# A transformer block with a dynamic convolution on one core: a second norm's squares on another engine, and two taps behind a variance

## The chip, the cores and the metric

The kernel runs on one core of one Trainium2 chip. The metric is the device time of one execution in microseconds. The time before is 3081.14 us, the median of three runs (3079.3 to 3084.65). The core's engines appear in profiles as PE (TensorE, matrix products; PEld are its weight loads), DVE (VectorE), ACT (ScalarE), POOL (GpSimd) and SP (SyncE, which issues the transfers here).

## The reference

The input is 16 images of 192 channels and 56 x 56 points, float32. Two layers follow each other. The first is a shifted-window transformer block, the second a depthwise convolution whose weights depend on the image:

```python
# layer 0, per point over the 192 channels
h = _ln(x, norm1_g, norm1_b)                 # first norm
h = attention in shifted 7 x 7 windows       # qkv, scores + bias + mask, softmax, values, projection
x1 = shortcut + h
y = _ln(x1, norm2_g, norm2_b)                # second norm: mean and variance over the channels
y = gelu(y @ fc1_w + fc1_b) @ fc2_w + fc2_b
x = x1 + y
# layer 1, per image
wt = (relu(bn(mean(x) @ w1.T)) @ w2.T + b2) * MASK      # four taps are left of the 3 x 3
out = depthwise_conv(x, wt) + bias
```

A norm needs, for each point, the sum over the channels and the sum of their squares.

## The kernel before

An image is worked off in four row groups of 2 x 7 rows, called steps, and the loop is pipelined: in loop step `i` the attention of step `i`, the MLP of step `i - 2`, the first norm's sums of step `i + 3` and the convolution of an older image run side by side. 128 channels lie on the partitions of one tile, the other 64 in a second tile (both row halves, one on each half of the partitions).

The sums over channels are matmuls with a selecting matrix (`st`). So that one matmul for each statistic is enough, the three pieces of the data are folded into one before: `own` is what already lies on the right partitions, the rest is copied over by two transfers into `xs[:, 1]`. The same for the squares, `s1` (the 64 channels), `s0[p, 0]` (own) and `s0[:, 1]` (copied):

```python
    def norm_folded(key, i, side):
        v0, v1 = flat_of(i)
        ...
        def copies():
            nc.sync.dma_start(xs[0:64, 1], v0[64:128, 0])
            nc.sync.dma_start(xs[64:128, 1], v0[0:64, 1])

        def sums():
            for p, h in own:
                nc.gpsimd.tensor_tensor(xs[p, 0], v0[p, h], v1[p], ALU.add)              # L274
            nc.gpsimd.tensor_tensor(xs[:, 0], xs[:, 0], xs[:, 1], ALU.add)               # L275

        def squares(engine):
            if engine is nc.gpsimd:
                nc.gpsimd.tensor_tensor(s1, v1, v1, ALU.mult)                            # L279
            else:
                nc.scalar.activation(s1, v1, AF.Square)                                  # L281
            return [
                lambda: [nc.scalar.activation(s0[p, 0], v0[p, h], AF.Square) for p, h in own],  # L283
                lambda: nc.scalar.activation(s0[:, 1], xs[:, 1], AF.Square),             # L284
            ]

        def fold():
            nc.gpsimd.tensor_tensor(s0[:, 0], s0[:, 0], s1, ALU.add)                     # L288
            nc.gpsimd.tensor_tensor(s0[:, 0], s0[:, 0], s0[:, 1], ALU.add)               # L289
```

The variance of both norms, made of the statistics in a PSUM bank pair:

```python
    def norm_vars(keys, st, tag="dev"):
        ...
        nc.scalar.activation(part, st[lo:hi, 0, :T], AF.Square)                          # L323
        nc.vector.tensor_tensor(part, st[64 + lo : 64 + hi, 0, :T], part, ALU.subtract)  # L324
```

The MLP's first layer has six groups of hidden channels on four bank pairs. Groups 0 to 2 take their wide products (128 channels) first and then the narrow ones (64 channels); groups 3 to 5 the other way round. `st` takes the bank pair of group 2, groups 4 and 5 those of 0 and 1, so each waits for the GELU that empties its bank pair:

```python
        for f in range(3):
            take(f); long(dsts[f], wf1, cols(f), y0, True)
        for f in range(3):
            short(dsts[f], wf1, cols(f), y1, False)
            gelu(f)                                                                      # L640
        after()
        for f in range(3, NFC):
            take(f); short(dsts[f], wf1, cols(f), y1, True)
        between()
        for f in range(3, NFC):
            long(dsts[f], wf1, cols(f), y0, False)
            gelu(f)
```

A convolution piece is begun by ScalarE with one tap and finished by VectorE with three (`tap` is L750). An image has six pieces, in four loop steps: one, two, two, one:

```python
    def conv_begin(b, wt, n, y=None):
        ...
        nc.scalar.activation(y, up, AF.Identity, bias=cb[kc], scale=wt[:, kc, 1:2])      # L742

    def conv_rest(b, wt, n, y, part=None):
        ...
        if part != 1:
            tap(0, y[:, :, 1:], up[:, :, : IMG - 1])
        if part == 0:
            return
        tap(2, y[:, :, : IMG - 1], up[:, :, 1:])
        if n in (3, 5):
            nc.vector.tensor_copy(...)                                                   # L762
        tap(3, y[:, :, 1:], cur[:, :, : IMG - 1])
        conv_store(b, n, y)
```

The loop step, cut to what the change touches and what stands around it (`first` is true in the step with an image's first piece, whose weights have only just been made):

```python
    for i in range(2, NS + 2):
        first = bool(convs) and not convs[0]["n"]
        cs = conv_ready(1 if first else 2)
        ys = [] if first else [conv_begin(*c) for c in cs[:1]]
        if has(i + 1):
            norm1_scale(i + 1, dvs.pop(0), nc.vector)        # win <- x, dv: L365, L373

        def after():
            ys.extend(conv_begin(*c) for c in cs[len(ys) :])
            for k, (c, y) in enumerate(zip(cs, ys)):
                conv_rest(*c, y, 0 if k else None)

        def between():
            st = banks(f"st_{i}", C)
            keys.update(stats_of(i, st))
            if keys:
                var.append(norm_vars(keys, st)[0])
            for c, y in zip(cs[1:], ys[1:]):
                conv_rest(*c, y, 1)
        ...
        mlp_first(i - 2, yns.pop(i - 2), hid, (A, B_, C, D, A, B_), after, between)
        ...
        top, share = attention_scores(i, *qs.pop(i), (C, D, A, B_))   # sc, and e <- sc, bias_t: L521
        qs[i + 1], outs = attention_qk(i + 1, C, D, A)                # pq, pe, pk
        ...
        if has(i):
            residual(i, pp, pair1, at)
            copies, sums_, squares, fold = norm_folded(f"2_{i}", i, 1)   # second norm
            copies()
            rest = squares(nc.gpsimd)
            sums_()
        if has(i + 1):
            v_whole()
            attention_v_out(pvs)                             # vbd <- pv on VectorE and ScalarE: L493
        if has(i):
            for f in rest:
                f()
            fold()
```

Of the kernel before, what the change touches and what calls it, by code (L numbers as in the profile page):

```python
# [9 lines left out]
AF = mybir.ActivationFunctionType  # L10
ALU = mybir.AluOpType
# [25 lines left out]
def tile_swin_then_dynamic_conv(  # L37
# [31 lines left out]
    nc = tc.nc  # L69
# [163 lines left out]
    def flat_of(i):  # L233
        v0, v1 = rows_of(i)
        return v0.rearrange("p h r c -> p h (r c)"), v1.rearrange("p r c -> p (r c)")
# [23 lines left out]
    def norm_folded(key, i, side):  # L259


        v0, v1 = flat_of(i)
        xs = one.tile([128, 2, T], F32, tag=("xs", "o")[side], name=f"xs_{key}")
        s0 = one.tile([128, 2, T], F32, tag=f"sq0{side}", name=f"sq0_{key}")
        s1 = one.tile([128, T], F32, tag=f"sq1{side}", name=f"sq1_{key}")
        own = [(slice(h * 64, h * 64 + 64), h) for h in range(2)]
# [8 lines that stand above are left out]
            nc.gpsimd.tensor_tensor(xs[:, 0], xs[:, 0], xs[:, 1], ALU.add)  # L275

        def squares(engine):
            if engine is nc.gpsimd:
                nc.gpsimd.tensor_tensor(s1, v1, v1, ALU.mult)  # L279
            else:  # L280
                nc.scalar.activation(s1, v1, AF.Square)  # L281
            return [
                lambda: [nc.scalar.activation(s0[p, 0], v0[p, h], AF.Square) for p, h in own],  # L283
                lambda: nc.scalar.activation(s0[:, 1], xs[:, 1], AF.Square),  # L284
            ]

        def fold():
            nc.gpsimd.tensor_tensor(s0[:, 0], s0[:, 0], s1, ALU.add)  # L288
            nc.gpsimd.tensor_tensor(s0[:, 0], s0[:, 0], s0[:, 1], ALU.add)  # L289

        xss[key] = xs[:, 0], s0[:, 0]
        return copies, sums, squares, fold
# [438 lines left out]
    def piece_of(b, n):  # L731


        kc, lo = (0, n * PR) if n < 4 else (1, (n - 4) * PR)
        xk = images[b][kc]
        return kc, lo, xk[:, lo : lo + PR], xk[:, lo + 1 : lo + 1 + PR]
# [8 lines left out]
    def conv_rest(b, wt, n, y, part=None):  # L745

        kc, _, up, cur = piece_of(b, n)

        def tap(t, dst, src):
            nc.vector.scalar_tensor_tensor(  # L750
                dst, src, wt[:, kc, t : t + 1], dst, ALU.mult, ALU.add
# [9 lines that stand above are left out]
            p = slice(0, 128) if kc == 0 else slice(64, 128)  # L761
            nc.vector.tensor_copy(  # L762
                y[p, LAST - 3 * PR, :], cb[kc][p].broadcast_to([p.stop - p.start, IMG])
            )
        tap(3, y[:, :, 1:], cur[:, :, : IMG - 1])
        conv_store(b, n, y)
# [37 lines left out]
    def conv_ready(k):  # L804

        ready = []
        while k and convs and "wt" in convs[0]:
            c = convs[0]
            ready.append((c["b"], c["wt"], c["n"]))
            c["n"] += 1  # L810
            k -= 1
            if c["n"] == 6:
                convs.pop(0)
        return ready
# [35 lines left out]
    for h in range(2):  # L850
        p = slice(h * 64, h * 64 + 64)
# [140 lines left out]
    for h in range(2):  # L992
        p = slice(h * 64, h * 64 + 64)
# [77 lines left out]
    v_whole()  # L1071
    copies, sums_, squares, fold = norm_folded("1_4", 4, 0)
    copies()
    for f in squares(nc.scalar):
        f()
    sums_()
    yns[0] = norm2_scale(0, dvs.pop(1), True)
    fold()
# [5 lines left out]
    residual(1, pp, pair1)  # L1084
    copies, sums_, squares, fold = norm_folded("2_1", 1, 1)
    copies()
    for f in squares(nc.gpsimd):
        f()
    sums_()
    fold()  # L1090
    nc.vector.reciprocal(s, s)
    nc.vector.tensor_tensor(s, s, g, ALU.mult)
# [10 lines left out]
    for i in range(2, NS + 2):  # L1103
        A, B_, C, D = pairs
        keys = {}
# [7 lines that stand above are left out]
            norm1_scale(i + 1, dvs.pop(0), nc.vector)  # L1113

        def after():
            ys.extend(conv_begin(*c) for c in cs[len(ys) :])
            for k, (c, y) in enumerate(zip(cs, ys)):
                conv_rest(*c, y, 0 if k else None)

        if (i + 3) % STEPS == 0 and (i + 3) // STEPS < B:  # L1120
            b = (i + 3) // STEPS
            images[b] = load_x(b, nc.sync)

        def between():
            st = banks(f"st_{i}", C)
            keys.update(stats_of(i, st))
            if keys:
                var.append(norm_vars(keys, st)[0])
            for c, y in zip(cs[1:], ys[1:]):
                conv_rest(*c, y, 1)  # L1130

        var = []
        hid = one.tile([128, NFC, 2, T], F32, tag="hid", name=f"hid_{i - 2}")
        mlp_first(i - 2, yns.pop(i - 2), hid, (A, B_, C, D, A, B_), after, between)
        for part in var:
            table(AF.Sqrt)
            norm_root(part)

        if has(i + 3):
            copies, sums_, squares, fold = norm_folded(f"1_{i + 3}", i + 3, 0)  # L1140
            copies()


        outs = [lambda: None] * 4
        if has(i):
            table(AF.Exp)
            top, share = attention_scores(i, *qs.pop(i), (C, D, A, B_))
        if has(i + 1):
            qs[i + 1], outs = attention_qk(i + 1, C, D, A)
        if has(i):  # L1150
            top(0)
        outs[0]()
        if has(i):
            top(1)
            share(0)
        outs[1]()
        if has(i):
            top(2)
            share(1)
        outs[2]()  # L1160
        if has(i):
            top(3)
            share(2)
        outs[3]()
        if has(i):
            share(3)
        for part in var:
            nc.vector.reciprocal(part, part)
            dvs.update(norm_spread(keys, part))

        prts = []

        def turn(f):
            for wp in ((), (), (), (0,), (1,), (2, 3))[f]:
                if has(i):
                    prts.append(attention_turn(i, wp, (C, A)[wp % 2]))

        pf = mlp_wide(i - 2, hid, B_, turn)  # L1180
        mlp_out(i - 2, 0, pf[:, :, :T])
        table(AF.Gelu)
        if has(i + 3):
            sums_()
        if 1 in keys:
            yns[i - 1] = norm2_scale(i - 1, dvs.pop(1), i == NS)
        if has(i):
            o = attention_rows(i, attention_values(i, prts, D, C))
        if has(i + 3):
            for f in squares(nc.scalar):  # L1190
                f()
            fold()
        pf1 = mlp_narrow(i - 2, hid, A)
        mlp_out(i - 2, 1, pf1[:, :T])
        if has(i):
            pp, pair1, p_narrow, p_rest, p_whole = project(i, o, B_, C)
            p_narrow()
            p_rest()
        if has(i + 1):
            pvs, v_rest, v_whole = attention_v(i + 1, (D, A))  # L1200
            v_rest()
        if has(i):
            p_whole()
        b, pt, at = (i - 2) // STEPS, None, lambda: None
        if (i - 2) % STEPS == STEPS - 1:
            pt = taps(b, taps_pool(b), pair1[:, 1] if has(i) else banks(f"t_{b}", C)[:, 0])
            convs.append({"b": b, "n": 0})

            def at():
                convs[-1]["tt"] = taps_hidden(b, pt)  # L1210

        if has(i):
            residual(i, pp, pair1, at)
            copies, sums_, squares, fold = norm_folded(f"2_{i}", i, 1)
# [4 lines that stand above are left out]
            at()  # L1219
        if has(i + 1):  # L1220
            v_whole()
            attention_v_out(pvs)
        if has(i):
            for f in rest:
                f()
            fold()
        if pt is not None:
            taps_rows(b, nc.scalar.copy if i > NS else nc.vector.tensor_copy)
            convs[-1]["wt"] = taps_out(b, convs[-1]["tt"])
        pairs = [C, B_, D, A]  # L1230

    c = convs.pop()
# [92 lines left out]
```

## Time and profile before

| | before |
|---|---|
| time, median of 3 | 3081.14 us |
| span of the profiled execution | 3081.5 us |
| granted TensorE clock, mean | 0.994 |
| ScalarE square of the copied channels, L284 | 123 times, 65.2 us, mean 530 ns |
| GpSimd square of the 64 channels, L279 | 63 times, 52.8 us, mean 839 ns |
| VectorE tap, L750 | 282 times, 286.4 us, mean 1025 ns |
| variance on VectorE, L324, in the loop | 60 times (64x392 form), 34.2 us, mean 570 ns |

The busy table gives each engine's busy time and its share of the span; shares are averages over stages with different limits. A row of the waits reads: the engine and tile that sat idle, what ended the idle time, microseconds in total, number of times, the longest. A row of the timeline reads: start and duration in microseconds, engine, line of the kernel, operation, what it writes and reads, and how many like instructions are merged into it; in brackets stand the idle time ahead of it and what ended that. All matmuls are issued from one helper line, L87, so they are told apart by their tiles: `ph` is the MLP's first layer, `pf` its second, `st` the statistics, `sc` the scores, `pq`, `pe` and `pk` the queries and keys.

### The profile page before, as it was taken

How to read it: one execution, taken by the hardware profiler on the slowest of the kernel's cores; microseconds unless marked ns; L12 is line 12 of the kernel's file. 1: busy time of each engine (PE TensorE's matmuls, PEld its weight loads, DVE VectorE, ACT ScalarE, POOL GpSimd, SP SyncE). 2: the span in 40 equal slices, each digit the busy share in tenths (PEclk: the TensorE clock that was granted, in tenths of full speed). 3: DMA queues.
4: the chain of work that ended last, by engine and by line, in shares of the span. 5: the costliest groups of instructions: out<-in, count | busy, mean ns of one | idle time of the engine just before them, and what ended most of it. 6: DMA issues, size and time to landing. Idle time of an engine off the chain costs nothing.

```text
span 3081.5 us, 62245 instructions
## 1 busy us (share of the span) xinstructions
PE 3048.0 (99%) x25182; PEld 1893.6 (61%) x25182; DVE 2116.0 (69%) x3828; ACT 1987.8 (65%) x3230; POOL 1273.1 (41%) x1209
## 2 busy tenths in 40 slices
PE   8999999999999999999999999999999999999998
PEld 5566666666666666666666666666666666666654
DVE  5665776766766766866867767667667668668664
ACT  4666766766766766766667667667667667666553
POOL 5434334344344344344343343343443443443421
PEclk8999999999999999999999999999999999999999
DMA  4002121121211112121121211212111121211101
GB/s 110 30 22 61 46 69 35 51 64 40 68 47 42 59 46 72 38 64 49 43 67 46 69 35 51 64 41 71 44 43 59 46 71 38 65 47 43 33 30 55
DMA packets 68264, 159.90 MB, mean 52 GB/s; under 512 B 11186, under 2 KB 34456, under 8 KB 66056
## 3 DMA queue, kind: packets, MB, share of 16 engines
q1 hardware_dynamic: 66302, 154.05, 16.6%
q8 instruction: 199, 3.26, 0.4%
q0 software_dynamic: 1360, 1.26, 0.3%
q14 instruction: 89, 0.73, 0.1%
q10 hardware_dynamic: 314, 0.59, 0.1%
HBM read 92.24 MB, written 38.93 MB: 43 GB/s over the span
## 4 chain that ended last, share of the span: by engine, by line
PE 90%; DVE 7%; issue 1%; ACT 0%; DMA 0%; POOL 0%; POOLq 0%; DVEq 0%; ACTq 0%
PE pf L87 24%; PE ph L87 21%; PE pp L87 8%; PE pv L87 7%; PE po L87 6%; PE pq L87 5%; PE pt L550 5%; PE sc L87 4%; PE pk L87 4%; PE pe L87 4%; DVE vbd L493 1%; PE st L87 1%; DVE win L365 1%; DVE win L373 1%; DVE y L750 1%
## 5 line engine op out<-in xcount | busy, mean ns | idle before, releaser
L87 PE MATMUL ph<-yn,wf 128*128 128x392 f32 (+1 forms) x3072 | 812.4, 504 | 0.3 <-DVE x L626 0.3
L87 PE MATMUL pf<-hid,wf 128*128 128x392 f32 (+1 forms) x3072 | 802.9, 494 | 3.5 <-ACT hid L640 2.0
L537 POOL TENSOR_TENSOR prob<-e,tot 113x588 f32<-113x588 f32 x256 | 297.6, 1173 | 1118.8 <-DVE tot L536 1118.7
L87 PEld LDWEIGHTS ph<-yn,wf 128*128 128x128 f32 (+1 forms) x3072 | 418.2, 188 | 366.3 <-issue 76.5
L87 PEld LDWEIGHTS pf<-hid,wf 128*128 128x128 f32 (+1 forms) x3072 | 386.5, 164 | 303.6 <-issue 119.8
L493 ACT COPY vbd<-pv 49x192 f32<-49x192 f32 x512 | 160.1, 313 | 568.7 <-DVE vbd L493 564.2
L686 DVE SCALAR_TENSOR_TENSOR x<-pf,cols,x 128x784 f32<-128x784 f32 (+1 forms) x128 | 106.2, 830 | 520.0 <-PE pf L87 443.1
L640 ACT ACTIVATE hid<-ph,f1b 128x784 f32<-128x784 f32 x384 | 336.9, 913 | 129.3 <-PE ph L87 127.8
L750 DVE SCALAR_TENSOR_TENSOR y<-x,wt,y 128x770 f32<-128x770 f32 x282 | 286.4, 1025 | 17.3 <-ACT y L742 8.9
L87 PEld LDWEIGHTS pv<-wqkv,win 64*128 64x128 f32 (+1 forms) x2048 | 255.4, 188 | 30.9 <-issue 1.2
L87 PE MATMUL pv<-wqkv,win 64*128 64x192 f32 (+1 forms) x2048 | 272.3, 325 | 0.0
L528 DVE TENSOR_TENSOR e<-e,top 113x588 f32<-113x588 f32 x256 | 262.3, 1025 | 8.9
L274 POOL TENSOR_TENSOR xs<-x,x 64x392 f32<-64x392 f32 x246 | 248.9, 1012 | 35.4 <-DVE x L626 26.2
L556 ACT COPY prt<-pt 128x678 f32<-128x678 f32 x256 | 179.2, 726 | 118.5 <-PE pt L550 117.0
L87 PE MATMUL pp<-o,wp 128*128 128x392 f32 (+2 forms) x896 | 251.4, 514 | 0.0
L521 DVE TENSOR_TENSOR e<-sc,bias_t 113x588 f32<-113x588 f32 x256 | 179.6, 763 | 104.0 <-PE sc L87 103.7
L241 ACT ACT_TABLE_LOAD x192 | 246.3, 1283 | 5.3 <-issue 1.8
L531 ACT ACTIVATE e<-e 113x588 f32<-113x588 f32 x256 | 176.8, 691 | 102.8 <-DVE e L528 102.8
L389 POOL TENSOR_TENSOR yn<-x,dv 128x784 f32<-128x784 f32 x62 | 115.6, 1865 | 235.0 <-DMA dv<-rows 235.0
L550 PEld LDWEIGHTS pt<-ident,prob 113*128 113x128 f32 x1536 | 165.5, 141 | 65.4 <-issue 36.1
L87 PE MATMUL po<-prt,vbd 128*64 128x49 f32 x6144 | 197.1, 223 | 0.4 <-ACT prt L556 0.4
L87 PEld LDWEIGHTS po<-prt,vbd 128*64 128x64 f32 x6144 | 188.9, 138 | 9.7 <-ACT prt L556 0.6
(176 smaller groups left out, 4372.9 us busy)
## 6 DMA issues: line engine op xcount, KB each, us to landing
dv<-rows SPq DMA_DIRECT2D x127, 392.0 KB
xs<-x SPq DMA_DIRECT2D x246, 98.0 KB
x<-in_x_dram SPq DMA_DIRECT2D x15, 1484.0 KB
out_dram<-y SPq DMA_DIRECT2D x48, 392.0 KB
out_dram<-y SPq DMA_DIRECT2D x48, 196.0 KB
x<-in_x_dram SPq DMA_DIRECT2D x16, 392.0 KB
x<-in_x_dram SPq DMA_DIRECT2D x15, 350.0 KB
out_dram<-y SPq DMA_DIRECT2D x16, 308.0 KB
```

The costliest lines, as they stand in the source:

```text
L87: nc.tensor.matmul(dst, lhs, rhs, start=start, stop=stop, skip_group_check=True)
L241: nc.scalar.activation(junk, eps_t[0:1], func)
L274: nc.gpsimd.tensor_tensor(xs[p, 0], v0[p, h], v1[p], ALU.add)
L493: copy(dst, src[s * 64 : s * 64 + N, h, :, :, j, :])
L521: nc.vector.tensor_tensor(e, sc[:PW, :, : HEADS * N], rel, ALU.add)
L528: nc.vector.tensor_tensor(ehs[wp], ehs[wp], t.broadcast_to([PW, 2 * HEADS, N]), ALU.subtract)
L531: nc.scalar.activation(es[wp], es[wp], AF.Exp)
L537: nc.gpsimd.tensor_tensor(prob[wp][:PW, :, 0:N], ehs[wp], t.broadcast_to([PW, 2 * HEADS, N]), ALU.mult)
L550: nc.tensor.transpose(pt[:, a, g * PW : (g + 1) * PW], prob[wp][:PW, h : h + 2, :].rearrange("p h k -> p (h k)"), ident[:PW, :PW],)
L556: nc.scalar.copy(prt, pt[:, :, : 3 * PW])
L640: nc.scalar.activation(hid[:, f], phs[f][:, :, :T], AF.Gelu, bias=f1b[:, f : f + 1])
L750: nc.vector.scalar_tensor_tensor(dst, src, wt[:, kc, t : t + 1], dst, ALU.mult, ALU.add)
```

## The change

The square of the copied channels, `s0[:, 1]`, goes to the engine that `squares` is called with. For the second norm that is GpSimd instead of ScalarE; it stands behind the sums and ahead of the fold there. For the first norm it stays on ScalarE, but the copied half now comes ahead of the own halves. It is meant to take work off ScalarE between the attention's copies and the GELUs.

In the step with an image's first convolution piece, only one of VectorE's three taps is made ahead of the variance; the other two and the store come behind it, as it was done for the second piece of other steps. It is meant to free the statistics' bank for the scores sooner.

```diff
         def squares(engine):
-            if engine is nc.gpsimd:
-                nc.gpsimd.tensor_tensor(s1, v1, v1, ALU.mult)
-            else:
-                nc.scalar.activation(s1, v1, AF.Square)
-            return [
-                lambda: [nc.scalar.activation(s0[p, 0], v0[p, h], AF.Square) for p, h in own],
-                lambda: nc.scalar.activation(s0[:, 1], xs[:, 1], AF.Square),
-            ]
+            def those_of(dst, src):
+                if engine is nc.gpsimd:
+                    nc.gpsimd.tensor_tensor(dst, src, src, ALU.mult)
+                else:
+                    nc.scalar.activation(dst, src, AF.Square)
+
+            those_of(s1, v1)
+
+            def rest():
+                those_of(s0[:, 1], xs[:, 1])
+                for p, h in own:
+                    nc.scalar.activation(s0[p, 0], v0[p, h], AF.Square)
+
+            return rest
@@ in the prologue @@
-    for f in squares(nc.scalar):
-        f()
+    squares(nc.scalar)()
@@
-    for f in squares(nc.gpsimd):
-        f()
+    rest = squares(nc.gpsimd)
     sums_()
+    rest()
     fold()
@@ in after() and between() @@
             for k, (c, y) in enumerate(zip(cs, ys)):
-                conv_rest(*c, y, 0 if k else None)
+                conv_rest(*c, y, 0 if k or first else None)
@@
-            for c, y in zip(cs[1:], ys[1:]):
+            for c, y in list(zip(cs, ys))[0 if first else 1 :]:
                 conv_rest(*c, y, 1)
@@ first norm, then second norm, in the loop @@
-            for f in squares(nc.scalar):
-                f()
+            squares(nc.scalar)()
             fold()
@@
-            for f in rest:
-                f()
+            rest()
             fold()
```

## The prediction

> **What bounds the kernel now.** I read the busy table first, then the totals of the waits, then the timeline of one loop step of each kind.
>
> ```profile
> PE 3048.0 (99%) x25182; PEld 1893.6 (61%) x25182; DVE 2116.0 (69%) x3828; ACT 1987.8 (65%) x3230; POOL 1273.1 (41%) x1209
> ```
>
> TensorE bounds nearly everything. The change takes no matmul away, so it can only win where TensorE waits. From one load of the `st` weights (the norm statistics) to the next, a step of the timeline lasts 46.4 to 46.9 us. Among the waits three totals concern the change:
>
> ```profile
> POOL sq L288 <- ACT sq L283: 120.1, 61, 2.1
> PEld ph L87 <- ACT hid L640: 53.5, 116, 0.5
> PEld sc L87 <- DVE dev L324: 11.0, 15, 1.0
> ```
>
> The first says that GpSimd idles some 2 us a step for ScalarE's squares. The second is two waits in each of 58 steps: the first layer of the MLP needs banks that a GELU on ScalarE has yet to empty. The third is 15 waits, one per image: the scores need the bank that the variance still reads. The idle times also hold pauses that are there without any wait, so I compare steps instead of adding them. First ScalarE and the weight loads in a step with two pieces of convolution:
>
> ```profile
> 1518.00 1.07 ACT L283 ACTIVATE sq<-x 64x392 f32<-64x392 f32 x2
> 1518.77 2.28 PEld L87 LDWEIGHTS ph<-yn,wf 64*128 64x128 f32 x16 [0.56 <-issue]
> 1519.09 0.53 ACT L284 ACTIVATE sq<-xs 128x392 f32<-128x392 f32 x1
> 1519.53 1.02 ACT L742 ACTIVATE y<-x,cols,wt 128x784 f32<-128x784 f32 x1
> 1520.58 2.52 ACT L640 ACTIVATE hid<-ph,f1b 128x784 f32<-128x784 f32 x3
> 1521.54 0.30 PEld L87 LDWEIGHTS ph<-yn,wf 64*128 64x128 f32 x4 [0.50 <-ACT hid L640]
> 1522.35 0.30 PEld L87 LDWEIGHTS ph<-yn,wf 64*128 64x128 f32 x4 [0.50 <-ACT hid L640]
> 1523.20 0.11 PEld L87 LDWEIGHTS st<-xs,sel 128*32 128x32 f32 x2 [0.56 <-ACT hid L640]
> ```
>
> ScalarE is busy without a gap from the squares to the GELUs, and the loads of MLP groups 4 and 5 start 0.05 us behind the GELUs that free their banks. From the first narrow load (1518.77) to `st` (1523.20) it takes 4.43 us. An early step, before any image is finished, has no L742:
>
> ```profile
> 210.56 3.59 PEld L87 LDWEIGHTS ph<-yn,wf 64*128 64x128 f32 x24 [0.56 <-issue]
> ...
> 211.57 2.52 ACT L640 ACTIVATE hid<-ph,f1b 128x784 f32<-128x784 f32 x3 [0.15 <-PE ph L87]
> ...
> 214.71 0.11 PEld L87 LDWEIGHTS st<-xs,sel 128*32 128x32 f32 x2 [0.56 <-ACT hid L640]
> ```
>
> All 24 loads run through in one piece and it takes 4.15 us, with the same 0.56 pause in front of `st`. So ScalarE costs 4.43 - 4.15 = 0.28 us a step. The `st` loads at 168.35 and 214.71 stand 46.36 us apart, those at 1523.20 and 1569.86 46.66: the same difference. A first GELU is possible 1.01 us after the first narrow load (211.57 - 210.56); in the busy step it comes after 1.81.
>
> [...]
>
> ```profile
> 1519.06 1.15 DVE L373 TENSOR_TENSOR win<-x,dv 64x28 f32<-64x28 f32 x2
> 1519.14 1.02 POOL L288 TENSOR_TENSOR sq<-sq,sq 128x392 f32<-128x392 f32 x1 [2.05 <-ACT sq L283]
> 1520.23 1.10 DVE L365 TENSOR_TENSOR win<-x,dv 128x21 f32<-128x21 f32 x2
> 1520.24 1.04 POOL L289 TENSOR_TENSOR sq<-sq 128x392 f32<-128x392 f32 x1
> ```
>
> Two tiny multiplies that take 0.29 us when GpSimd is idle (L365 at 1518.86, the same 28 columns) take 1.15 and 1.10 beside L288 and L289, and each pair ends just behind the GpSimd instruction. [...] The trace has the very operation, a 128x392 square, as L279: 839 ns (two different inputs: 1,031 ns, L288).
>
> **The change part by part.**
>
> *Squares moved.* Per step, one ScalarE square of 530 ns (L284) becomes a GpSimd multiply of 839 ns. There are 63 second norms (L279 x63): ScalarE loses 63 x 0.530 = 33 us, GpSimd gains 63 x 0.839 = 53 us. GpSimd queues it behind L275, which ends at 1517.09, inside the 2.05 us of idle time ahead of L288, so the fold should still end near 1521.5 and `st` at about 1522.9 has its input.
>
> *What ScalarE gives back.* L742 and the GELUs move up by 0.53 us. The first GELU then stands 1.81 - 0.53 = 1.28 us behind the first narrow load; that is later than 1.01, so TensorE is ready for it. The second ends at 1.28 + 0.80 + 0.91 = 2.99, the load of group 5 needs it at about 3.08. So the narrow phase falls to 4.15 us: **-0.28 us** in steps whose GELUs stand behind an L742. In the step with an image's first piece there is no L742 ahead of the GELUs; it takes 4.22 us (1612.51 to 1616.73), so -0.06.
>
> *What VectorE loses.* The new GpSimd square starts at about 1517.17, beside L365 and L373. [...] the square ends at about 1518.16. The second L365 is blocked that long and ends at about 1518.53 instead of 1517.90. [...] I get the end of the `win` chain at 1522.29 instead of 1521.61: **+0.68 us** on VectorE.
>
> Whether this reaches TensorE depends on the step. Each image has four; the idle time of VectorE ahead of its four score additions L521 says how much room there is:
>
> - One last piece: 3.43 us of room (1575.67). Nothing lost, -0.28.
> - Pieces 1 and 2: 0.61 us (1669.38). With TensorE 0.28 earlier and VectorE 0.68 later the additions come 0.35 us late. A step of the trace has just that lateness: additions at 828.16, 1.23 us behind the scores' first load instead of the usual 0.87. There the narrow `pk` loads come 0.14 later than in an undisturbed step (830.34 - 826.93 = 3.41 against 1671.77 - 1668.50 = 3.27), and the wide `pq` loads 4.35 behind that first load in both (831.28, 1672.85). So this is free: -0.28.
> - Pieces 3 and 4: 0.38 us (1529.02), as the copy L762 takes 0.2. The additions come 0.68 - (0.38 - 0.28) = 0.58 late. Four narrow loads take 0.52 us when they run ahead and 0.30 when they had to wait, so 0.22 of a wait at `pk` is hidden; 0.35 of lateness made 0.14, so 0.43 makes 0.22, and 0.58 - 0.43 = 0.15 is lost: -0.13.
> - First piece: next part.
>
> *Taps behind the variance.* Now VectorE makes three taps, 1618.07 to 1621.20, and then the variance, to 1621.80:
>
> ```profile
> 1618.07 3.13 DVE L750 SCALAR_TENSOR_TENSOR y<-x,wt,y 128x770 f32<-128x770 f32 x3
> 1621.23 0.57 DVE L324 TENSOR_TENSOR dev<-st,dev 64x392 f32<-64x392 f32 x1
> 1621.86 2.05 PEld L87 LDWEIGHTS sc<-kbd,q 64*64 64x64 f32 x96 [0.74 <-DVE dev L324]
> ```
>
> The scores start 5.13 us behind `st` (1616.73), elsewhere 4.94: 0.19 lost. With two taps of 1.04 us behind the variance, it ends some 2.1 us sooner, and the wait goes[...]. The taps then end near 1622.3; the additions are wanted near 1622.5. [...] So -0.06 - 0.17 = -0.23.
>
> *Sum.* Per image -0.28 - 0.28 - 0.13 - 0.23 = -0.92 us. There are 59 loop steps with pieces, 15 of each kind but 14 last ones: 15 x 0.64 + 14 x 0.28 = **13.5 us** less, 3081.1 to 3067.6, or 0.44%. The first norm's order (copied half before own halves, still on ScalarE) and the prologue I count as nothing: the same four squares stand ahead of the same GpSimd fold.
>
> **The rivals.** (1) [...] If VectorE loses 0.9 to 1.0 us a step instead of 0.68, both kinds of two-piece step get no gain or a loss of 0.2, and only the other two win: about 15 x 0.3 = 5 us. For it: the neighbouring adds of the chain show a full instruction's block each. Against it: the square is short (839 ns)[...]. (2) *Nothing moves because TensorE is busy 99%.* Against it: the steps with and without L742 differ by 0.29 us with the same matmuls. (3) *More than planned*: if [...]VectorE loses under 0.5 us, all kinds reach the undisturbed length: 14 x 0.28 + 30 x 0.28 + 15 x 0.23, about 16 us, 3065. (4) *The GpSimd fold becomes the last input of `st`*: it has more than 1 us of room (1521.5 against 1522.9), so unlikely.
>
> **Range and chances.** The ways above end between 3065 and about 3078; the three timed runs of before spread over 5 us. I take 3067.5, with 3062 to 3079 to hold it 8 times in 10. A change of 2% would be 62 us, four times what ScalarE's part can free at most, and a loss of 62 us would be a whole microsecond in every step; neither is in sight: 0.005 each.
>
> **What would show it.** After the change the `ph` waits for ScalarE should nearly go from the totals and the narrow phase should be 4.15 us in every kind; the `sc` waits for the variance should be gone; L365 and L373 should be longer by some 0.7 us a step, and the waits of VectorE's additions for scores should vanish in two-piece steps. If instead `pk` or `pq` loads wait for L521 in most steps, rival 1 holds. The prediction is wrong if GpSimd's square does not start where I put it (behind L275)[...].

## The result and the profile after

The changed kernel takes 3066.13 us (median of six runs, 3064.43 to 3067.48), the kernel before 3079.7 us (six runs, 3078.48 to 3084.65). The ratio is 0.9954, with a 95% interval from 0.9941 to 0.9967: 13.6 us or 0.44% less. The line numbers behind the changed function have moved, mostly by six: the squares on GpSimd, old and new, are now L280, the own squares L289, the folds L294 and L295, `win` L371 and L379, GELU L646, a piece's begin L748, taps L756, the variance L330, the score additions L527.

The busy table of the changed kernel:

```profile
PE 3034.7 (99%) x25182; PEld 1900.7 (62%) x25182; DVE 2147.0 (70%) x3828; ACT 1951.8 (64%) x3167; POOL 1346.6 (44%) x1272
```

The work went where it was sent: 63 instructions fewer on ScalarE and 36 us less, 63 more on GpSimd and 73.5 us more. VectorE has the same 3828 instructions and is busy 31 us longer (2147.0, was 2116.0): what GpSimd costs it is inside its instructions' durations and not in its idle time. Of the 31 us, 18 lie in two small instructions of the first-piece steps that now run beside the square and the fold: a copy of 64x56 (L706) takes 0.78 instead of 0.19 us, an addition of 128x8 (L734) about 0.8 instead of 0.17. Most of the rest, 10.3 us, is in the `win` multiplies (341.1 us, were 330.8). TensorE's share, 99% in both, says nothing again; the totals of the waits of the changed kernel do:

```profile
POOL sq L294 <- ACT sq L289: 61.9, 59, 1.6
...
PEld ph L87 <- POOL sq L280: 29.6, 53, 0.6
...
PEld ph L87 <- ACT hid L646: 10.1, 45, 0.3
...
PEld pk L87 <- DVE e L527: 5.6, 17, 0.4
```

GpSimd's idle time ahead of the fold is halved (61.9 us, was 120.1), as it has the square to make there. The MLP's waits for GELUs fell from 53.5 us in 116 to 10.1 us in 45. Of the row `sc` for the variance, 15 waits and 11.0 us before, one of 0.6 is left. The row with GpSimd's L280 looks like a new wait of TensorE's and is none: each is the 0.56 us pause ahead of the first narrow load that stood under "issue" before (76.5 us in 128 waits then, 47.5 in 76 now; the difference of 29 us is the new row). The last row is new and real, and it is the price: narrow `pk` loads wait for VectorE's additions, nearly always in the steps with pieces 3 and 4.

In a two-piece step before, no GpSimd instruction ran beside the second of the first two `win` multiplies:

```profile
1516.63 1.27 DVE L365 TENSOR_TENSOR win<-x,dv 128x343 f32<-128x343 f32 x2
```

The timeline of one step with pieces 3 and 4 of the changed kernel, the counterpart of the first step shown before:

```profile
1694.92 1.92 DVE L371 TENSOR_TENSOR win<-x,dv 128x343 f32<-128x343 f32 x2
1695.35 1.11 POOL L280 TENSOR_TENSOR sq<-xs 128x392 f32<-128x392 f32 x1
...
1697.06 2.94 PEld L87 LDWEIGHTS ph<-yn,wf 64*128 64x128 f32 x20 [0.56 <-POOL sq L280]
...
1698.45 2.52 ACT L646 ACTIVATE hid<-ph,f1b 128x784 f32<-128x784 f32 x3
...
1700.05 0.36 DVE L379 TENSOR_TENSOR win<-x,dv 64x21 f32<-64x21 f32 x2
1700.22 0.43 PEld L87 LDWEIGHTS ph<-yn,wf 64*128 64x128 f32 x4 [0.23 <-ACT hid L646]
...
1701.21 0.11 PEld L87 LDWEIGHTS st<-xs,sel 128*32 128x32 f32 x2 [0.56 <-ACT hid L646]
...
1706.15 2.05 PEld L87 LDWEIGHTS sc<-kbd,q 64*64 64x64 f32 x96 [0.56 <-issue]
...
1707.48 2.80 DVE L527 TENSOR_TENSOR e<-sc,bias_t 113x588 f32<-113x588 f32 x4
...
1709.66 0.30 PEld L87 LDWEIGHTS pk<-win,wqkv 64*128 64x128 f32 x4 [0.37 <-DVE e L527]
...
1710.52 0.63 PEld L87 LDWEIGHTS pq<-win,wqkv 128*128 128x128 f32 x3 [0.56 <-issue]
```

From the first narrow load to `st`, the narrow phase, it is 1701.21 - 1697.06 = 4.15 us, was 4.43: the length of the undisturbed early step. The first two `win` multiplies, the second of them beside the new square, take 1.92 us instead of 1.27. The chain of all twelve ends 1700.41 - 1697.06 = 3.35 us after the first narrow load, was 2.84: VectorE is 0.51 later. Its additions come 1.33 us behind the scores' first load instead of 0.87, and `pk` waits for them; but the wide `pq` loads come 4.37 behind that first load, where 4.35 is undisturbed. The lateness is almost wholly hidden.

The step with an image's first piece in the changed kernel:

```profile
1610.27 1.02 DVE L756 SCALAR_TENSOR_TENSOR y<-x,wt,y 128x770 f32<-128x770 f32 x1
1611.33 0.57 DVE L330 TENSOR_TENSOR dev<-st,dev 64x392 f32<-64x392 f32 x1
1611.93 2.08 DVE L756 SCALAR_TENSOR_TENSOR y<-x,wt,y 128x770 f32<-128x770 f32 x2
1613.43 2.05 PEld L87 LDWEIGHTS sc<-kbd,q 64*64 64x64 f32 x96 [0.56 <-DVE y L756]
```

One tap, the variance, two taps. The `st` load of this step is at 1608.49, so the scores start 4.94 us behind it, as in the other steps (only in the loop's first it is 5.62). The name in the bracket is that of an instruction still running when the scores start (1611.93 + 2.08 = 1614.01), so it released nothing; 0.56 us is the usual pause.

From one `st` to the next the steps have these mean lengths, by what is done in the step that begins the stretch (worked out from the traces; us):

| stretch from | before | after |
|---|---|---|
| first piece | 46.82 | 46.36 |
| pieces 1 and 2 | 46.65 | 46.36 |
| pieces 3 and 4 | 46.65 | 46.41 |
| last piece | 46.87 | 46.81 |
| an image (added before rounding) | 186.99 | 185.93 |

From the first `st` to the end the traces last 2959.47 us before and 2945.45 after, 14.0 less. Ahead of the first `st` even traces of one and the same kernel differ: it comes at 121.99 us before and at 120.19 after, but at 118.61 in a second trace of the changed kernel (e9). So the whole spans of two traces should not be subtracted from each other.

### The profile page after: what moved, and what is told of

Its sections match the earlier page's. It is cut to its first block, busy times and chain, and to the rows that moved or that the text cites. A ratio compares the mean times of both kernels' runs of the same rounds, so it can differ in the third digit from the quotient of the medians.

```text
span 3065.6 us, 62137 instructions
## 1 busy us (share of the span) xinstructions
PE 3034.7 (99%) x25182; PEld 1900.7 (62%) x25182; DVE 2147.0 (70%) x3828; ACT 1951.8 (64%) x3167; POOL 1346.6 (44%) x1272
## 4 chain that ended last, share of the span: by engine, by line
PE 97%; DVE 2%; ACT 0%; DMA 0%; issue 0%; POOL 0%; POOLq 0%; DVEq 0%; ACTq 0%
PE ph L87 26%; PE pf L87 25%; PE pv L87 8%; PE pp L87 8%; PE po L87 6%; PE pq L87 5%; PE pt L556 5%; PE sc L87 4%; PE pk L87 4%; PE pe L87 4%; PE st L87 2%; PE pc L87 0%; DVE e L534 0%; PE pb_p L87 0%; DVE vbd L499 0%
## 5 line engine op out<-in xcount | busy, mean ns | idle before, releaser
L87 PE MATMUL ph<-yn,wf 128*128 128x392 f32 (+1 forms) x3072 | 799.1, 497 | 0.3 <-DVE x L632 0.3
L87 PEld LDWEIGHTS ph<-yn,wf 128*128 128x128 f32 (+1 forms) x3072 | 426.7, 188 | 344.4 <-issue 47.5
L646 ACT ACTIVATE hid<-ph,f1b 128x784 f32<-128x784 f32 x384 | 336.9, 913 | 135.3 <-PE ph L87 133.8
L756 DVE SCALAR_TENSOR_TENSOR y<-x,wt,y 128x770 f32<-128x770 f32 x282 | 287.1, 1028 | 15.3 <-ACT y L748 7.0
L527 DVE TENSOR_TENSOR e<-sc,bias_t 113x588 f32<-113x588 f32 x256 | 179.6, 763 | 70.5 <-PE sc L87 69.3
```

Source lines behind the costliest of these rows:

```text
L87: nc.tensor.matmul(dst, lhs, rhs, start=start, stop=stop, skip_group_check=True)
L527: nc.vector.tensor_tensor(e, sc[:PW, :, : HEADS * N], rel, ALU.add)
L646: nc.scalar.activation(hid[:, f], phs[f][:, :, :T], AF.Gelu, bias=f1b[:, f : f + 1])
L756: nc.vector.scalar_tensor_tensor(dst, src, wt[:, kc, t : t + 1], dst, ALU.mult, ALU.add)
```

## The experiments

All kernels' times are medians of at least five runs; e1 to e4 ran on one chip beside the kernel before at 3079.74, e5 to e7 on one beside 3080.16, e8 and e9 on one beside 3080.43.

**e1: only the squares move.** The edit takes the changed kernel's taps back:

```diff
-                conv_rest(*c, y, 0 if k or first else None)
+                conv_rest(*c, y, 0 if k else None)
-            for c, y in list(zip(cs, ys))[0 if first else 1 :]:
+            for c, y in zip(cs[1:], ys[1:]):
```

> Only the squares move; all three taps of an image's first piece stay ahead of the variance. My theory (ScalarE frees the narrow phase[...]): the narrow phase is 4.15 us in every step as in the changed kernel, but in the step with an image's first piece [...]the scores start some 0.6 us late there: 15 x 0.6 = 9 us back, about 6 us under the kernel before (3074). Rival (the two parts are independent, the taps give their 0.19 us x 15 = 3 us alone): about 11 us under the kernel before (3069).

Measured: 3075.43 us, ratio 0.9985 (0.9979 to 0.9992), 4.3 us under the kernel before. The weight loads' waits in e1:

```profile
PEld sc L87 <- DVE dev L330: 18.5, 16, 1.3
```

This wait has grown from 11.0 us, and the scores of the first-piece step start 5.57 us behind `st` where the changed kernel has 4.94: 0.63 us, as expected, 15 times. The parts are not independent: moving the squares makes the variance late, and the second part pays for it.

**e2: only the taps move.** The kernel before, with the changed kernel's two lines for the taps.

> Only the taps move; the squares stay on ScalarE. My theory: 15 waits of the scores for the variance lose their 0.17 to 0.19 us each, about 3 us under the kernel before (3077), the narrow phase stays at 4.43 us in 44 steps. Rival (the taps carry most of the gain): 8 us or more under it.

Measured: 3077.74 us, ratio 0.9992 (0.9984 to 1.0), 2.0 us under the kernel before; the interval just reaches no difference, and the trace is clearer: `st` to scores 4.94 in all steps, the narrow phase unchanged at 4.44 and 4.21. Alone the parts give 4.3 and 2.0, together 13.6.

**e3: the square left out.** The second norm has neither the square of the copied channels nor the fold's second add, so its variance lacks 64 channels' part:

```diff
             def rest():
-                those_of(s0[:, 1], xs[:, 1])
+                if engine is not nc.gpsimd:
+                    those_of(s0[:, 1], xs[:, 1])
@@ fold @@
-            nc.gpsimd.tensor_tensor(s0[:, 0], s0[:, 0], s0[:, 1], ALU.add)
+            if side == 0:
+                nc.gpsimd.tensor_tensor(s0[:, 0], s0[:, 0], s0[:, 1], ALU.add)
```

> Leaves out the square of the copied channels and the second fold add of the second norm altogether (the variance is then wrong, the rest runs as it is). If TensorE's own stream is the bound in the changed kernel[...]: the same time as the changed kernel within 1 us (about 3065.5), with only the steps with pieces 3 and 4 shorter by some 0.02 us. Rival[...]: 3 us or more under the changed kernel.

Measured: 3064.16 us (3062.21 to 3064.82), ratio 0.9949 (0.9936 to 0.9961), 2.0 us under the changed kernel: between what the two theories named, nearer to the first. The trace splits it. Steps are 46.36, 46.36, 46.36 and 46.81 long, so the steps with pieces 3 and 4 gain 0.6 us in all, of which 0.4 is one step of the changed kernel's trace in which the copies into `xs` landed late; and in two places outside the regular steps it gains 0.7 us each, of which more below. Against the changed kernel VectorE's `win` chain is 1.3 us shorter in each two-piece step, and TensorE's steps hardly move: in the changed kernel's loop TensorE's own stream is the bound.

**e4: the first norm in its old order.**

```diff
+                if engine is nc.gpsimd:
                     those_of(s0[:, 1], xs[:, 1])
                 for p, h in own:
                     nc.scalar.activation(s0[p, 0], v0[p, h], AF.Square)
+                if engine is not nc.gpsimd:
+                    those_of(s0[:, 1], xs[:, 1])
```

> The changed kernel with the first norm's squares in the old order (own halves first, copied half last). My theory: no difference, 3066 within 1.5 us, since the same three squares end ahead of the same fold. Rival (the order of the first norm frees the fold and with it something that TensorE waits for): 3 us or more slower than the changed kernel.

Measured: 3066.21 us, ratio 0.9956 (0.9944 to 0.9969). No effect of that part of the change shows.

**e5: the square made twice on GpSimd.**

```diff
                 those_of(s0[:, 1], xs[:, 1])
+                if engine is nc.gpsimd:
+                    those_of(s0[:, 1], xs[:, 1])
```

> The changed kernel, with GpSimd making the moved square twice (the same values again): 0.84 us more of GpSimd reading beside VectorE's win multiplies. [...] VectorE some 0.8 us later in every step; room is left in the step with the last piece, none in the two-piece steps, which lose about 0.6 and 0.8 us, and some 0.2 us in the first-piece step by the later fold: about 3089, 23 us over the changed kernel. Rival (GpSimd, 44% busy, works beside the rest): only the fold's lateness in first-piece steps shows, about 3068.

Measured: 3083.18 us, ratio 1.0008 (1.0002 to 1.0015), 17 us over the changed kernel. The weight loads' waits in e5:

```profile
PEld pq L87 <- DVE e L529: 17.0, 28, 0.9
...
PEld pe L87 <- DVE e L529: 10.8, 29, 0.4
PEld pk L87 <- DVE e L529: 10.8, 29, 0.4
```

All three rows are VectorE's lateness, in 28 or 29 steps, the two-piece ones. There the `win` chain ends 0.64 us later than in the changed kernel (0.8 expected) and the stretches from there are 0.40 and 0.62 us longer (0.6 and 0.8 expected); last-piece and first-piece steps lose nothing. From the fifth `st` to the last the loop is 14.3 us longer, 14 steps of each kind; 4.5 us more came at its first stretch and behind the last `st`, which had not been expected: GpSimd's fold ends 1.58 and 2.61 us behind the `st` loads there, 0.64 in the changed kernel. So VectorE is held up by the second square too, as expected, and by less than was estimated.

**e6: memsets ahead of the square.** GpSimd first fills the square's output twice with zeros, two instructions of 0.43 us that only write:

```diff
+                if engine is nc.gpsimd:
+                    for _ in range(2):
+                        nc.gpsimd.memset(s0[:, 1], 0.0)
                 those_of(s0[:, 1], xs[:, 1])
```

> The changed kernel, with two memsets of the square's own output ahead of it on GpSimd: about 0.95 us more of GpSimd that only writes. If it is reading that blocks VectorE: win multiplies no longer than in the changed kernel, and the time 3066 to 3070 (the fold comes up to 0.2 us late in 15 first-piece steps). If any GpSimd instruction blocks VectorE, or if it is GpSimd's own queue that counts: as with the square made twice, about 3089.

Measured: 3066.44 us, ratio 0.9957 (0.9945 to 0.997): the changed kernel's time. In a two-piece step (the kernel's lines are three further down):

```profile
1692.62 1.28 DVE L374 TENSOR_TENSOR win<-x,dv 128x343 f32<-128x343 f32 x2
1693.04 0.90 POOL L289 MEMSET sq<- 128x392 f32 x2
```

The pair of multiplies that took 1.92 us beside the square takes 1.28 beside the memsets, and took 1.27 before the change. All `win` multiplies of a two-piece step add up to 5.80 us, against 5.90 in the changed kernel and 6.53 in e5. GpSimd was kept nearly as long as in e5 (the memsets took 0.90 us, e5's squares of the copied channels 1.00 each in the mean) and these multiplies were not blocked. So for the `win` multiplies, which have two inputs, it is the square, which reads, that costs (1.92 us), and neither GpSimd's time nor its queue (1.28 us beside the memsets).

For VectorE's copies that is not so. In the first-piece steps two of them run beside the memsets:

```profile
1600.61 0.94 DVE L708 COPY x<-x 128x56 f32<-128x56 f32 x1
1601.07 0.91 POOL L289 MEMSET sq<- 128x392 f32 x2
1601.56 0.47 DVE L709 COPY x<-x 64x56 f32<-64x56 f32 x1
```

In the changed kernel the first takes 0.57 us in this step; the second took 0.19 before the change, with GpSimd idle. Here each ends 0.04 to 0.05 us behind a memset, and this is so in 14 of 15 first-piece steps. So a GpSimd instruction that only writes does hold up these copies: 0.94 us instead of 0.57, 0.47 instead of 0.19. It cost no time: the stretch from the first-piece step stays at 46.36 us.

**e7: ScalarE's time given back.** One more square of the copied channels on ScalarE, into a scratch tile that nobody reads:

```diff
                     nc.scalar.activation(s0[p, 0], v0[p, h], AF.Square)
+                if engine is nc.gpsimd:
+                    nc.scalar.activation(scr, xs[:, 1], AF.Square)
```

> The changed kernel, with one more square of the copied channels on ScalarE, into a tile that nobody reads, at the place where the old one stood: ScalarE's time is given back, all else stays. If ScalarE's 0.44 to 0.53 us ahead of the GELUs are the whole gain of the first part: the narrow phase is 4.4 us again in the 44 steps with an L742 ahead, and 12 us of the gain are gone, about 3077.5. Rival (the gain came from what GpSimd's earlier fold or the dropped wait for the copies frees): near 3066.

Measured: 3078.91 us, ratio 0.9998 (0.999 to 1.0006): 12.8 us of the gain are gone. Its weight loads' waits:

```profile
PEld ph L87 <- ACT hid L649: 53.4, 116, 0.5
```

The same 116 waits as before the change, and the narrow phase is 4.44 us again. One square's time on ScalarE, at this one place, is the whole of the first part's gain.

**e8: the ends on ScalarE.** The traces showed where else the change costs something. At the first `st` of the changed kernel's loop:

```profile
120.19 0.11 PEld L87 LDWEIGHTS st<-xs,sel 128*32 128x32 f32 x2 [0.56 <-ACT hid L646]
...
120.88 0.14 PEld L87 LDWEIGHTS st<-sq,sel 128*32 128x32 f32 x2 [0.54 <-POOL sq L295]
```

The sums are there, the squares are not: GpSimd's fold ends 0.64 us behind the first load, where before it ended 0.44 ahead of it. The last `st` waits in the same way. e8 leaves the square on ScalarE for these two norms:

```diff
-        def squares(engine):
+        def squares(engine, copied=None):
...
-                those_of(s0[:, 1], xs[:, 1])
+                those_of(s0[:, 1], xs[:, 1], copied or engine)
...
-    rest = squares(nc.gpsimd)
+    rest = squares(nc.gpsimd, nc.scalar)
...
-            rest = squares(nc.gpsimd)
+            rest = squares(nc.gpsimd, nc.scalar if i == NS - 1 else None)
```

> The changed kernel, but with the copied channels' square on ScalarE in two places alone: the second norm of the prologue and that of the last step. In the changed kernel GpSimd's fold comes after the st matmuls want it there (the first st of the loop and the last one each wait, 0.68 and 0.69 us). My theory: both waits go, nothing else changes: 1.4 us under the changed kernel, about 3064.7. Rival (the late folds are hidden by what follows, or ScalarE becomes late there): the same as the changed kernel, 3066.

The changed kernel beside it, e9:

> The changed kernel once more, on the same chip as e8, so that the two can be compared: 3066 within 1.5 us by every theory.

Measured: e8 3065.14 us (3063.74 to 3066.89), ratio 0.995 (0.9936 to 0.9964); the changed kernel beside it 3066.04 us (3065.56 to 3066.51), ratio 0.9953 (0.9939 to 0.9967). The 0.9 us between the medians lie inside the spread of the runs. The traces show that the waits went: the first stretch of the loop is 46.36 us (47.04 in e9), from the last `st` to the end 68.11 (69.0). The rival was half right: in the last step ScalarE is late again, and the stretch ahead of the last `st` takes 40.96 us (40.69). From the first `st` to the end e8 lasts 2944.3 us and e9 2945.2. Of the kernels that compute the right result it is the best here, by about a microsecond that the times alone do not prove.

## Why the prediction was right, point by point

The predicted 3067.5 lies 1.4 us from the measured 3066.1; as a gain it is 13.5 against 13.6 us. Its steps:

- **The narrow phase** was right: 4.15 us in every kind of step, and e7 shows that ScalarE's square alone sets it.
- **How far the GELUs move up** was mis-sized: the first now stands 1.39 us behind the first narrow load (1698.45 - 1697.06), so 0.42 and not 0.53 sooner. The duration of the removed instruction, 0.53 us, was taken. Back to back, it started 0.44 us ahead of the next (1519.09, 1519.53), and about that is what its removal gives. The rest of its 0.53 us, 0.09, overlaps with the next instruction (1519.09 + 0.53 = 1519.62). The mis-sizing cost nothing, as the narrow phase came out at 4.15 us all the same, but the MLP's waits for ScalarE fell to 10.1 us rather than to nearly none.
- **VectorE's delay** was right in kind and too large: 0.51 us in two-piece steps instead of 0.68. The 0.68 was the author's estimate from the trace before: a multiply was taken to be held until the GpSimd instruction running beside it ends, as in the two pairs that took 1.15 and 1.10 us. Behind the four wide multiplies it is 0.66 (1697.80 - 1697.06 against 1518.85 - 1518.77), close to the 0.63 worked out for the second of them; among the small ones 0.15 is won back. Between GpSimd's two folds two small multiplies get through (at 1698.64 and 1698.74, 0.18 and 0.17 us long), where before the change one did (1520.23). VectorE's additions no longer wait for the scores in these steps, as foretold (35 such waits in all, 63 before). So the steps with pieces 3 and 4 lose 0.01 to 0.02 us to late additions, not 0.15 (0.05 in the mean, with the one step in which the copies into `xs` landed late).
- **GpSimd's own cost** was too small: 73.5 us more, not 53. The moved square took 1.11 us in three steps of four, where 0.84 had been taken for all, and the folds of both norms are 9.7 us longer in sum. In the loop's other steps this stayed free, with the fold ahead of `st` by 0.7 us or more (once 0.15).
- **The hidden 0.22 us at `pk`** was right. A step whose additions are 0.42 us late goes on at its normal time, one with 0.47 loses 0.03 (the steps of the changed kernel with `st` at 771.3 and 585.4 us); 0.43 had been worked out as the limit.
- **The taps** were right: the scores' 0.16 us in first-piece steps came back, and e1 shows the 0.63 us that VectorE's lateness would have cost there.
- **The sum** came out by two misses of opposite sign, and that they cancel is luck. The regular steps gave 15.3 us, from the fifth `st` to the last, instead of 13.5, mostly because VectorE's delay was smaller; in the loop it is nearly rival 3 (about 16 us) that came true. Against that, 0.68 us in the loop's first stretch and 0.7 at its end were lost. This is rival 4, a fold that becomes the last input of `st`: it was dismissed on a regular step's room of over 1 us (it was 0.76 in the first-piece steps, which was enough). At the loop's first `st` the room before the change was 0.44 us, and at the last one the 1.07 us were not enough: at both the fold now ends 0.64 us behind the load. 15.3 - 1.4 = 13.9.

Rival 1 was one GpSimd instruction away: e5 is about what it describes, with the stretches of two-piece steps 0.11 and 0.38 us longer than before the change.

## What to carry to other kernels

Before giving work to GpSimd, look at what VectorE does at that moment. GpSimd's busy share, 41% before, told nothing here. The first pair of `win` multiplies, with two inputs, took 1.92 us beside a square, which reads, and 1.28 beside memsets, which only write; a copy of 64x56 took 0.19 us with GpSimd idle, 0.78 beside the square, and 0.47 beside the memsets, too. The cost appeared in VectorE's durations, 31 us in sum. Where TensorE is busy 99% of the time, compare a step that has the suspected work ahead of TensorE's next bank with one that doesn't, and take each kind of step for itself, the first and the last too. When a move makes one engine late and another early, look for the second edit that turns the lateness away from the path; tried one by one, the two parts here gave 6.3 us of 13.6.

## What the hardware showed that was not expected

A GpSimd multiply of 128x392 took 839 ns with one tensor as both inputs, an addition of two tensors 1,031 ns (L279 and L288 before), and 1,013 ns in the 29 cases with no VectorE instruction beside it. The second tensor and not the operation seems to make the difference, since a multiply of two tensors of 64x392 took 1,020 ns (L393 before). In the changed kernel the moved square kept the shorter time, 0.84 us, in the first-piece steps, and took 1.11 us in the 46 cases in which a `win` multiply ran beside it. A blocked VectorE multiply of 28 columns, 0.18 us long when GpSimd is idle, ended about 0.05 us behind the GpSimd instruction that blocked it (1520.21 behind 1520.16 before); one of 343 columns, 0.51 us long when GpSimd is idle, ended 0.38 us behind (1696.84 behind 1696.47 after).
